# The edge loops of stages 1 and 5, staggered by a pair of groups and issued in written order

## The chip, the cores and the metric

The kernel runs on one core of a Trainium2 chip. A core has engines that each run their own stream of instructions in order: TensorE (PE: matmuls, and PEld: its weight loads), VectorE (DVE), ScalarE (ACT), GpSimd (POOL) and SyncE (SP). POOL issues the indirect DMAs (gathers and scatters) here, SP and ACT the plain DMAs. The metric is device microseconds of one launch of the whole program. The edge loops that are changed are two parts of it.

## The reference, cut to what matters

Eight stages run one after the other on 6250 nodes (49 tiles of 128) and a graph of 100000 edges: four graph layers (stages 1, 3, 5, 7), each followed by an expert layer (stages 2, 4, 6, 8). Stage 4's graph has 131072 edges of its own. The edges of stages 1 and 5 are sorted by their target node `dst`. Stage 1 is attention with 4 heads of 64 columns, stage 5 has one head of 256 columns. For each target node both compute a softmax over its edges and a weighted sum of rows of the source nodes:

```
stage 1:  s[e,h] = sum_c q[dst[e],h,c] * k[src[e],h,c] / 8        value row v[src[e]]
stage 5:  s[e]   = leaky(a_src[src[e]] + a_dst[dst[e]] + a_e[e])  value row z[src[e]]
m[n]   = max over e with dst[e] = n of s[e]
p[e]   = exp(s[e] - m[dst[e]])
out[n] = sum p[e] * value[src[e]] / sum p[e]
```

## The kernel before, in words

**Windows.** `windows` (called once) cuts the sorted edges into NW = 112 groups ("windows") of GE = 896 = 7 x 128 edges. A window's first target is `n0`; the targets of its edges lie in `n0` to `n0 + 127` (the seldom case that they do not is handled by `further`, behind a condition). An edge's `lane` is its target minus `n0`. The tables kept in SBUF are `idx` (source nodes), `lane` and `isl` (1 where an edge is the last of its target in the window); in DRAM `laned` (lanes), `rfd` and `rrd` (a very negative number where a target starts, forward and backward) and `isd`.

**The edge loop** is `att_windows` (line 625), used by stage 1 (line 947, table `kvd`, 512 columns) and stage 5 (line 1711, table `zd`, 257 columns). It goes over 56 pairs of windows, `g = 0, 2, ...`:

- `begin` (647): SP loads the lanes, broadcast to all partitions (`lr`); DVE compares them with the partition number to `ohT` (target by edge, bf16, line 745) and builds `oh` (edge by target, bf16, both windows in one instruction, line 654); SP loads the four reset rows `rst`. Then for each window POOL gathers 7 x 128 rows into `roww` (line 603), and `front` makes the scores. In stage 1 `front` (930) spreads the targets' `q` over the edges by 21 matmuls with `ohT` (`qe`, 938), multiplies into the row (941) and reduces (942). In stage 5 (1697) 7 small matmuls `de` do this for one number per target.
- `middle` (672): the scores of both windows are transposed to rows (681, 682: once forward and once reversed), copied by ACT to `sT` (683), and one DVE scan (685) makes running maxima over each target, forward and backward. They are transposed back (688), the backward half turned by 7 matmuls with `flip` (694); the larger of the two is the target's maximum `mxw`. `p` is the exp of the difference (699). `p` goes behind the row's 256 value columns (702), and the maximum times `isl` behind that (703): a sum over a target's edges then delivers its maximum.
- `end` (707): each of the 7 blocks of a row is scaled by `p`, 5 by ACT (715, one instruction per head) and 2 by DVE (718); ACT casts `oh` to f32 `ow` (721); 7 matmuls (725, two passes each in f32) sum the window into one PSUM tile `ops`; ACT copies it out (`osb`, 728); SP stores lanes 1 to 127 to `main` and lane 0 to `part` (749, 750).

For each pair the program calls `begin` and `middle` of the pair and then `end` of the pair before. The order of the instructions on POOL is the written one (`tc.manual_schedule` with POOL alone); on PE, DVE, ACT and SP a scheduler orders them. `roww` has 5 buffers in stage 1 and 6 in stage 5. `att_join` (829) afterwards adds the lane-0 rows of `part` to `main`, with the maxima that stand in the rows' last columns.

**The steps.** `bucket_move` (line 146) sorts another edge list into buckets; it is a generator that yields between small pieces ("steps"). Stage 1 calls it for `sb` (100000 edges, BT = 4) and advances it 3 steps for each window, with the rest after the loop; stage 3 calls it for `sc` (131072 edges, BT = 6), one step for each of 448 chunks. Its phases: counting (49 buckets; compare `isb` and matmul, 224), positions (49 buckets; compare, three matmuls 300 and 302, masked copy 304), moving (groups of columns; per step the one-hots `ol` (321) and `orr` (323, 326) and BT matmuls `mv` (329); at the end of a group some 12 small instructions and 16 scatters by POOL, line 365, 4 a step), and reading back (376 to 389).

## Time and profile before

| what | us |
|---|---|
| median of 3 runs | 11532.18 (11513.21 to 11543.58) |
| the profiled execution | 11636.83 |
| its span in the profile | 11635.0 |
| mean granted TensorE clock | 0.699 of full |
| PE busy | 6837.3 (59%) |
| DVE busy | 5143.1 (44%) |
| POOL busy | 4453.4 (38%) |
| ACT busy | 2537.3 (22%) |

The profile is one execution of the program, recorded by the hardware. Its span is what lies between the first and the last recorded instruction; the profiled execution's own time is the span and 1.8 us around it. An engine's busy time counts its data instructions alone. The clock is what the throttle granted to TensorE; at a lower clock the same matmul takes longer. "Idle before" in a group of instructions is the time its engine stood still just before them, with what released it. [...]

### The profile page before, as it was taken

Reading aid. Unit: us, or ns where it says so; the run is one execution under the profiler, and the core shown is the slowest. Engines: PE = TensorE matmul, PEld = TensorE weight load, DVE = VectorE, ACT = ScalarE, POOL = GpSimd, SP = SyncE. Lnnn points to the kernel's source line nnn. Section 1 sums busy time; section 2 is a strip of 40 time slices with the busy share of each in tenths; the row PEclk is TensorE's granted clock in tenths of the full one; section 3 lists DMA queues with packets and bytes.
Section 4 is the critical chain, followed back from the end, with each engine's and each line's share of the span. In section 5 each row is a group of like instructions: output and inputs, shape, how many; then the busy total and the mean of one; then the engine's idle time right before and its main releaser. Section 6 shows DMA issues by size and latency. Waiting matters only on the chain. (4 is left out here: it accounts for less than half of the span.)

```text
span 11635.0 us, 111114 instructions
## 1 busy us (share of the span) xinstructions
PE 6837.3 (59%) x33823; PEld 4547.9 (39%) x33823; DVE 5143.1 (44%) x14128; ACT 2537.3 (22%) x6685; POOL 4453.4 (38%) x4496
## 2 busy tenths in 40 slices
PE   4787666624866876554555555693455553562295
PEld 2444444423652333333333332481344442351263
DVE  5556565666224655414555555414222223624304
ACT  1344344421222000001111111131233332121021
POOL 0344445410133666662444443123444442053211
PEclk9878777765988766655655555797666666586597
DMA  3444444432653433351000000274333332273122
GB/s 131 160 134 127 133 132 121 133 110 97 204 175 106 119 94 96 108 133 35 7 6 6 6 6 6 89 218 122 94 90 88 88 88 69 87 218 55 47 71 72
DMA packets 613608, 1129.18 MB, mean 97 GB/s; under 512 B 156007, under 2 KB 419750, under 8 KB 598910
## 3 DMA queue, kind: packets, MB, share of 16 engines
q0 software_dynamic: 234752, 600.19, 19.4%
q1 hardware_dynamic: 320159, 454.55, 12.9%
q10 hardware_dynamic: 58060, 66.90, 1.8%
q8 instruction: 284, 4.65, 0.2%
q14 instruction: 353, 2.89, 0.1%
HBM read 930.68 MB, written 190.55 MB: 96 GB/s over the span
## 5 line engine op out<-in xcount | busy, mean ns | idle before, releaser
L603 POOL DMA_INDIRECT roww<-kvd,saidx x784 | 828.3, 1057 | 1145.9 <-ACT osb L728 459.8
L603 POOL DMA_INDIRECT row<-gatd,scsl x864 | 828.2, 959 | 1072.5 <-DVE pv L1463 290.8
L603 POOL DMA_INDIRECT roww<-zd,saidx x784 | 748.0, 954 | 1024.4 <-ACT osb L728 613.5
L603 POOL DMA_INDIRECT row<-w1d,sbsl x896 | 890.0, 993 | 626.7 <-PE nbp L1021 239.3
L725 PE MATMUL ops<-roww,ow 128*128 128x264 f32 (+1 forms) x3136 | 1064.1, 482 | 60.7 <-ACT osb L728 20.2
L715 ACT ACTIVATE roww<-roww,pw 128x64 f32<-128x64 f32 (+1 forms) x2800 | 808.4, 368 | 48.3 <-issue 46.1
L1021 PE MATMUL nbp<-row,sel 128*128 128x256 bf16 x2688 | 586.4, 369 | 382.7 <-DMA row<-w1d,sbsl 222.8
L725 PEld LDWEIGHTS ops<-roww,ow 128*128 128x128 f32 x3136 | 688.3, 238 | 272.2 <-issue 57.5
L1423 DVE TENSOR_REDUCE Mc<-P 128x4 f32<-128x1024 f32 x432 | 520.4, 1221 | 433.6 <-remote 315.0
L938 PE MATMUL qe<-qw,ohT 128*128 128x256 bf16 x2352 | 423.9, 332 | 397.9 <-DVE roww L941 343.0
L329 PE MATMUL mv<-orr,ol 128*128 128x234 f16 (+1 forms) x1824 | 545.1, 444 | 145.6 <-DVE orr L326 108.2
L1021 PEld LDWEIGHTS <-sel 128*128 128x128 bf16 x2688 | 377.5, 155 | 634.6 <-issue 424.2
L1419 PE MATMUL P<-identb,mb 128*128 128x512 bf16 x864 | 473.6, 570 | 190.7 <-issue 66.7
L688 PE MATMUL sm<-ident,sc 64*128 64x64 f32 x784 | 96.2, 283 | 819.1 <-DVE sc L685 756.3
L1260 PE MATMUL yp<-wr,hr 128*128 128x256 f32 x2176 | 535.8, 386 | 52.3 <-DVE yr L1263 52.3
L1298 PE MATMUL hp<-xr,wr 128*128 128x256 f32 x2176 | 534.7, 397 | 27.2 <-ACT hr L1300 19.9
L1057 PE MATMUL tps<-ident,xn 128*128 128x128 f32 x490 | 125.5, 404 | 685.8 <-DVE xn L124 469.8
L1422 PE MATMUL P<-rb,sel 96*128 96x512 bf16 x864 | 471.5, 568 | 89.9 <-DVE rb L1413 76.0
L1263 DVE TENSOR_TENSOR yr<-yp,br 128x256 f32<-128x256 f32 x328 | 138.9, 424 | 859.5 <-PE yp L1260 802.2
L941 DVE TENSOR_TENSOR roww<-roww,qe 128x512 f32<-128x512 f32 x448 | 270.7, 615 | 476.3 <-DMA roww<-kvd,saidx 213.5
L938 PEld LDWEIGHTS <-ohT 128*128 128x128 bf16 x2352 | 262.4, 116 | 535.8 <-issue 303.3
L685 DVE TENSOR_TENSOR_SCAN sc<-rst,sT 64x896 f32<-64x896 bf16 x112 | 225.9, 2017 | 552.3 <-ACT sT L683 503.4
(582 smaller groups left out, 14260.9 us busy)
## 6 DMA issues: line engine op xcount, KB each, us to landing
wr<-in_moe_dram SPq DMA_DIRECT2D x108, 1026.0 KB
lr<-salaned SPq DMA_DIRECT2D x112, 448.0 KB
yd<-yr SPq DMA_DIRECT2D x164, 256.0 KB
wr<-in_moe_dram SPq DMA_DIRECT2D x56, 513.0 KB
eat<-in_edge_attr_dram ACTq DMA_DIRECT2D x32, 781.2 KB
qw<-qd SPq DMA_DIRECT2D x112, 192.0 KB
br<-in_L_ffn_b_dram SPq DMA_DIRECT2D x164, 128.0 KB
main<-osb SPq DMA_DIRECT2D x112, 131.0 KB
```

Of the source, the lines that this page charges most:

```text
L329: nc.tensor.matmul(mv, ol[:, :, i], orr[:, 0:2, :, i], start=(c + i == c0), stop=(c + i == c0 + n - 1))
L603: return self.nc.gpsimd.indirect_dma_start(out=out, out_offset=None, in_=table, in_offset=bass.IndirectOffsetOnAxis(ap=idx, axis=0))
L715: nc.scalar.activation(x, x, AF.Copy, scale=p[:, j, i * H + h:i * H + h + 1])
L725: nc.tensor.matmul(ps[:, :VW], ow[:, j, :], row[:, j, v0:v0 + VW], start=(j == 0), stop=(j == BW - 1))
L938: nc.tensor.matmul(ps[:, b], ohT[:, j + b, :], qw[:, k], start=(k == 0), stop=(k == 2))
L941: nc.vector.tensor_mul(kr, kr, ps[:, :m])
L1021: nc.tensor.matmul(ps, sel[:, :, 2 * (c % G) + k], row[:, j * D:(j + 1) * D], start=(k + j == 0), stop=(k == 1 and j == 2))
L1260: nc.tensor.matmul(yp, hT[:, k, i * 128:(i + 1) * 128], w[:, O2 + k * D:O2 + (k + 1) * D], start=(k == 0), stop=(k == KH - 1))
L1298: nc.tensor.matmul(hp, w[:, k * H + m * 128:k * H + (m + 1) * 128], xe[:, k], start=(k == 0), stop=(k == 1))
L1419: nc.tensor.matmul(P[:, k], mb[:, :, 2 * i + k], self.identb.unsqueeze(1).to_broadcast([128, 4, 128]), start=True, stop=False)
L1422: nc.tensor.matmul(P[:, k], sel[:, 2 * i + k, :], rb, start=False, stop=True)
L1423: nc.vector.tensor_reduce(mg[:, i, :], P.rearrange("p k h e -> p h k e"), AX.XY, ALU.max)
```

## The change

**The loop's order.** `begin` is split into the loads (`begin`, now only SP), the lane one-hots (`lanes`) and the gathers with the scores of one window (`first`); `middle` into `turned` (transposes and `sT`), `scan` and `weigh`; `end` into `scaled` and `sums`. The main loop calls them so that scan, weights and sums of pair k-1 stand inside the iteration of pair k, between the scores of its two windows, and the loads for pair k+1 are issued in it too. `turned` of pair k ends the iteration. All five engines now issue in written order (`ORDERED`). Stage 1 has 6 row buffers. `qw` and `dw` are loaded by `load` with the pair, in 3 and 4 buffers.

**p on the one-hots.** In stage 5 the row is no longer scaled. DVE builds `ow` in f32 from the lane, times `p`, in 7 instructions a window; a column of ones in the table `zd` (now 258 wide) delivers the sum of `p`. In stage 1 ACT scales all 7 blocks and DVE builds `ow` in f32 with one compare. The bf16 `oh` and the cast go.

**Maxima.** Instead of carrying every target's maximum through the sums, the maximum of the first edge and of the last edge of each window is kept in `mfl` and stored once (`ends`). `main` and `part` become narrower, `isl` and `isd` go. `att_join` finds by a matmul with `bef` the maximum of the target that ends a window. The backward half of the scan is transposed back by itself, in reversed order, so that a single matmul turns it.

**The steps.** They are advanced by `tick` at 15 places a pair in stage 1: before each of the four groups of `qe` in both windows, once in `weigh`, and after every second block of `sums`. In `bucket_move` positions yield twice a bucket and the masked copy is put off by one piece; the end of a group is cut into more steps; the scatters are put off and go out one a step; reading back has more steps. This holds for stage 3 too, which otherwise is unchanged.

The diff, cut to its core:

```diff
+ORDERED = {mybir.EngineType.Pool, mybir.EngineType.PE, mybir.EngineType.DVE,
+           mybir.EngineType.Activation, mybir.EngineType.SP}
...
                 for j in range(2):
                     nc.tensor.matmul(big[:, :n], idt[:NT, j, b:b + 1].to_broadcast([NT, 128]),
                                      first[:, j, h:h + n], start=False, stop=(j == 1))
-                nc.vector.copy_predicated(pos[:, h:h + n], q.bitcast(I16), big[:, :n])
-            yield
+                if held is not None:
+                    nc.vector.copy_predicated(*held)
+                held = (pos[:, h:h + n], q.bitcast(I16), big[:, :n])
+                yield
+        nc.vector.copy_predicated(*held)
...
+        late = []
+
+        def scatter(n):
+
+            for _ in range(min(n, len(late))):
+                ti, vt, j = late.pop(0)
+                s = nc.gpsimd.indirect_dma_start(
+                    out=sld, out_offset=bass.IndirectOffsetOnAxis(ap=ti[:W, j:j + 1], axis=0),
+                    in_=vt[:W, 8 * j:8 * j + 8], in_offset=None, bounds_check=NB * 16 - 1,
+                    oob_is_err=False)
+                tc.declare_no_dep(s.ins, group=nm + "sc", reason="each piece has slots of its own")
+                tc.add_to_no_dep_group(nm + "sc", s.ins)
+
...
                 for i in range(k):
                     nc.tensor.matmul(mv, ol[:, :, i], orr[:, 0:2, :, i], start=(c + i == c0),
                                      stop=(c + i == c0 + n - 1))
+                if c > c0:
+                    scatter(1)
                 yield
...
+            st["node"] = [load(r, wp) for r in q["n0"]]
             return st
 
-        def middle(st):
-
-            n, s, q = st["n"], st["s"], st["q"]
-            m = n * H
-            sT = wp.tile([64, GE], F, name="sT", bufs=1)
+        def lanes(st):
+            st["ohT"] = wp.tile([128, 2 * BW, 128], BF, name="ohT")
+            st["q"]["ohT"](st["ohT"].rearrange("p b e -> p (b e)"), st["lr"])
+
+        def first(st, i, half=lambda: None):
+
+            row = gp.tile([128, BW, max(gw, v0 + VW)], F, name="roww")
+            for j in range(BW):
+                self.gather(row[:, j, :gw], tab, st["q"]["idx"](i, j))
+            front(st, i, row, st["ohT"][:, i * BW:(i + 1) * BW], st["s"][:, :, i * H:(i + 1) * H],
+                  wp, sp, tick, half)
+            st["row"].append(row)
+
+        def turned(st):
+
+            s = st["s"]
+            sT = st["sT"] = wp.tile([64, GE], F, name="sT", bufs=1)
             for j0, j1 in ((0, 4), (4, BW)):
                 ps = pm.tile([64, 512], F, name="sm")
                 for j in range(j0, j1):
...
                     nc.tensor.matmul(ps[0:32, o], s[:, j], self.ident, start=True, stop=True)
                     nc.tensor.matmul(ps[32:64, o], s[:, BW - 1 - j], self.flip, start=True, stop=True)
                 nc.scalar.activation(sT[:, j0 * 128:j1 * 128], ps[:, :(j1 - j0) * 128], AF.Copy)
...
+        def scan(st):
+
+            sc = st["sc"] = wp.tile([64, GE], F, name="sc", bufs=1)
+            nc.vector.tensor_tensor_scan(sc, st["rst"], st["sT"], NEG, op0=ALU.add, op1=ALU.max)
+
+        def weigh(st):
+
+            n, s, q, sc = st["n"], st["s"], st["q"], st["sc"]
+            m = n * H
+
             zf = sp.tile([128, 2, BW, m], F, name="zf")
-            for h in range(2):
-                nc.scalar.activation(zf[:, h], zp[:, :, 32 * h:32 * h + m], AF.Copy)
+            for h, r in ((1, slice(32, 64)), (0, slice(0, 32))):
+                zp = pm.tile([128, BW, 32], F, name="sm")
+                for j in range(BW):
+                    nc.tensor.transpose(zp[:, j if h == 0 else BW - 1 - j, :],
+                                        sc[r, j * 128:(j + 1) * 128], self.ident[r, r])
+                nc.scalar.activation(zf[:, h], zp[:, :, 0:m], AF.Copy)
             zr = pm.tile([128, BW, m], F, name="sm")
-            for j in range(BW):
-                nc.tensor.matmul(zr[:, j, :], self.flip, zf[:, 1, BW - 1 - j, :], start=True, stop=True)
+            nc.tensor.matmul(zr, self.flip, zf[:, 1], start=True, stop=True)
+            tick()
             mx = sp.tile([128, BW, m], F, name="mxw")
             nc.vector.tensor_max(mx, zf[:, 0], zr)
-            p = sp.tile([128, BW, m], F, name="pw")
+            p = st["p"] = sp.tile([128, BW, m], F, name="pw")
             nc.vector.tensor_sub(p, s[:, :, 0:m], mx)
             nc.scalar.activation(p, p, AF.Exp)
-            for i in range(n):
-                row, hs = st["row"][i], slice(i * H, (i + 1) * H)
-                nc.vector.tensor_copy(row[:, :, v0 + 256:v0 + 256 + H], p[:, :, hs])
-                nc.vector.tensor_mul(row[:, :, v0 + 256 + H:v0 + VW], mx[:, :, hs],
-                                     q["isl"](i).unsqueeze(2).to_broadcast([128, BW, H]))
-            st["p"] = p
-
-        def end(st):
-
-            for i in range(st["n"]):
-                row, p = st["row"][i], st["p"]
+            for e, j in ((0, 0), (1, BW - 1)):
+                nc.vector.tensor_copy(mfl[:, e, q["at"]:q["at"] + n, :].rearrange("p n h -> p (n h)"),
+                                      mx[:, j, :])
+
+        def scaled(st, i):
+
+            row, p, lane = st["row"][i], st["p"], st["q"]["lane"](i)
+            ow = wp.tile([128, BW, 128], F, name="ow")
+            if H > 1:
+                nc.vector.tensor_tensor(ow, self.iota.unsqueeze(1).to_broadcast([128, BW, 128]),
+                                        lane.unsqueeze(2).to_broadcast([128, BW, 128]), ALU.is_equal)
+                nc.vector.tensor_copy(row[:, :, v0 + 256:v0 + VW], p[:, :, i * H:(i + 1) * H])
                 for j in range(BW):
-                    if j < BW - dve:
-                        for h in range(H):
-                            x = row[:, j, v0 + h * C:v0 + (h + 1) * C]
-                            nc.scalar.activation(x, x, AF.Copy, scale=p[:, j, i * H + h:i * H + h + 1])
-                    else:
-                        x = row[:, j, v0:v0 + 256].rearrange("p (h c) -> p h c", h=H)
-                        nc.vector.tensor_mul(x, x, p[:, j, i * H:(i + 1) * H].unsqueeze(2).to_broadcast(
-                            [128, H, C]))
-                ow = wp.tile([128, BW, 128], F, name="ow")
-                nc.scalar.activation(ow, st["oh"][:, :, i * BW:(i + 1) * BW].rearrange("p n j -> p j n"),
-                                     AF.Copy)
-                ps = po.tile([128, 512], F, name="ops")
+                    for h in range(H):
+                        x = row[:, j, v0 + h * C:v0 + (h + 1) * C]
+                        nc.scalar.activation(x, x, AF.Copy, scale=p[:, j, i * H + h:i * H + h + 1])
+            else:
                 for j in range(BW):
-                    nc.tensor.matmul(ps[:, :VW], ow[:, j, :], row[:, j, v0:v0 + VW], start=(j == 0),
-                                     stop=(j == BW - 1))
-                o = wp.tile([128, VW], F, name="osb")
-                nc.scalar.activation(o, ps[:, :VW], AF.Copy)
-                st["q"]["put"](i, o)
-
-        pid = self.pid
-        held, regs = None, None
-        for g in range(0, NW, 2):
+                    nc.vector.tensor_scalar(ow[:, j], self.iota, lane[:, j:j + 1], p[:, j, i:i + 1],
+                                            op0=ALU.is_equal, op1=ALU.mult)
+            st.setdefault("ow", []).append(ow)
+
+        def sums(st, i):
+
+            row, ow = st["row"][i], st["ow"][i]
+            ps = po.tile([128, 512], F, name="ops")
+            for j in range(BW):
+                nc.tensor.matmul(ps[:, :VW], ow[:, j, :], row[:, j, v0:v0 + VW], start=(j == 0),
+                                 stop=(j == BW - 1))
+                if j % 2:
+                    tick()
+            o = wp.tile([128, VW], F, name="osb")
+            nc.scalar.activation(o, ps[:, :VW], AF.Copy)
+            st["q"]["put"](i, o)
...
+        held, nxt = None, windows(0)
+        lanes(nxt)
+        for g in range(0, NW, 2):
+            st = nxt
+            first(st, 0, (lambda: scan(held)) if held is not None else (lambda: None))
+            if g + 2 < NW:
+                nxt = windows(g + 2)
             if held is not None:
-                end(held)
+                weigh(held)
+                scaled(held, 0)
+            if st["n"] > 1:
+                first(st, 1)
+            if held is not None:
+                if held["n"] > 1:
+                    scaled(held, 1)
+                for i in range(held["n"]):
+                    sums(held, i)
+            turned(st)
+            if g + 2 < NW:
+                lanes(nxt)
             held = st
-        end(held)
+        scan(held)
+        weigh(held)
+        for i in range(held["n"]):
+            scaled(held, i)
+            sums(held, i)
         for _ in steps:
             pass
+        for e, r in ((0, slice(0, 1)), (1, slice(127, 128))):
+            nc.sync.dma_start(ends[e:e + 1], mfl[r, e, 0:NW, :])
...
+        bef = wp.tile([NW, NW], F, name="ajbe")
+        nc.vector.tensor_scalar(bef, t[:NW, :NW], S["lastf"], None, op0=ALU.is_equal)
+        nc.vector.tensor_tensor(bef, bef, eq, ALU.is_gt)
...
+            def load(n0, wp):
+                qw = wp.tile([128, 3, D], BF, name="qw", bufs=3)
+                nc.sync.dma_start(qw, qd[ds(n0, 128), :].rearrange("p (j d) -> p j d", j=3))
+                return qw
+
+            def front(st, i, row, ohT, s, wp, sp, tick, half):
+                qw = st["node"][i]
                 for j in range(0, BW, 2):
+                    tick()
+                    if j == 4:
+                        half()
                     m = min(2, BW - j)
                     ps = pq.tile([128, 2, D], F, name="qe")
                     for b in range(m):
...
                                         AX.X, ALU.add)
 
             steps = other(cx)
-            with tc.manual_schedule(engines={mybir.EngineType.Pool}):
-                self.att_windows(cx, S, kvd, 512, 4, 256, front, main, part, rows=5, steps=steps, per=3)
+            with tc.manual_schedule(engines=ORDERED):
+                self.att_windows(cx, S, kvd, 512, 4, 256, load, front, main, part, ends, rows=6, steps=steps)
...
+                    z = wp.tile([128, 258], F, name="z")
+                    nc.scalar.activation(z[:, 1:257], zp[:, D:], AF.Copy)
+                    nc.vector.memset(z[:, 257:258], 1.0)
                     for i, o in enumerate((z[:, 0:1], DD[:, t:t + 1])):
```

## The prediction

> **What bounds the kernel now.** I read the table of busy time by stretch first, cut at the first and last instructions on `roww`: the stage 1 edge loop runs from 380 to 2475 us, that of stage 5 from 8134 to 9811 us. Together they are 3772 of 11635 us; the rest is touched only in the helper `bucket_move`.
>
> ```profile
> core 0: us, PE busy (x) PEld busy (x) DVE busy (x) ACT busy (x) POOL busy (x), PEclk, DMA share, GB/s
> 380.00:2475.00 2095.00, 1436.24 (x7930) 958.45 (x7928) 1225.33 (x2550) 880.84 (x2765) 977.77 (x899) 0.76 0.44 131
> 8134.00:9811.00 1677.00, 860.88 (x5098) 705.61 (x5098) 381.14 (x1181) 544.59 (x1065) 747.99 (x784) 0.67 0.32 86
> ```
>
> No engine is full in either: 69% for PE in the first, 51% in the second. So both loops are chains of waits, not throughput. 56 pairs of windows: 2095/56 = 37.4 us and 1677/56 = 29.9 us a pair. Next, the waits inside 48 steady pairs of stage 5 (us in total, times, longest), and one pair in the timeline (start, us, engine):
>
> ```profile
> PEld sm L688 <- DVE sc L685: 667.0, 48, 14.9
> ...
> POOL roww L603 <- ACT osb L728: 569.0, 48, 12.2
> DVE e L1705 <- DMA roww<-zd,saidx: 432.0, 45, 14.0
> ```
> ```profile
> 8507.82 1.01 POOL L603 DMA_INDIRECT roww<-zd,saidx  x1 [11.90 <-ACT osb L728]
> ...
> 8524.12 0.95 POOL L603 DMA_INDIRECT roww<-zd,saidx  x1 [0.30 <-issue]
> 8527.82 0.48 ACT L683 ACTIVATE sT<-sm 64x384 f32<-64x384 f32 x1 [9.01 <-remote]
> ...
> 8528.34 2.02 DVE L685 TENSOR_TENSOR_SCAN sc<-rst,sT 64x896 f32<-64x896 bf16 x1 [8.46 <-ACT sT L683]
> ...
> 8530.41 1.00 PE L688 MATMUL sm<-ident,sc 64*128 64x64 f32 x7 [13.83 <-DVE sc L685]
> ...
> 8532.37 2.99 PE L694 MATMUL sm<-zf,flip 128*128 128x2 f32 x14
> ...
> 8537.17 1.01 POOL L603 DMA_INDIRECT roww<-zd,saidx  x1 [12.10 <-ACT osb L728]
> ```
>
> The reader sees a ring: 14 gathers at 0.95 + 0.30 us issue take 17.3 us (8507.82 to 8525.07); then the data, the scan, its transposes and 14 flips; only then do the old pair's last sums leave PE and free a row buffer for the next gather. 8537.17 - 8507.82 = 29.35 us, of which POOL idles 12. The gathers and the softmax take turns.
>
> Stage 1 has the same ring, but shares DVE and PE with `bucket_move` (lines 321 to 329), whose steps are slipped between its instructions by the scheduler. The groups of 700 to 2300 us (busy, mean ns) and a step as it ran:
>
> ```profile
> L603 POOL DMA_INDIRECT roww<-kvd,saidx x596 | 638.4, 1071 | 589.9 <-ACT osb L728 393.6 <-issue 163.7 <-ACT roww L715 22.1
> ...
> L329 PE MATMUL mv<-orr,ol 128*128 128x230 f16 x742 | 183.0, 383 | 35.7 <-DVE orr L326 25.1 <-issue 8.9
> L941 DVE TENSOR_TENSOR roww<-roww,qe 128x512 f32<-128x512 f32 x257 | 173.9, 681 | 325.3 <-DMA roww<-kvd,saidx 175.3 <-remote 123.6 <-PE qe L938 7.4
> L942 DVE TENSOR_REDUCE ss<-roww 128x28 f32<-128x1792 f32 x85 | 170.9, 2011 | 0.0
> ...
> L326 DVE TENSOR_TENSOR orr<-orr,v 128x460 f16<-128x460 f16 x362 | 150.0, 446 | 0.3
> ```
> ```profile
> 1500.39 7.74 ACT L715 ACTIVATE roww<-roww,pw 128x64 f32<-128x64 f32 x32
> ...
> 1505.51 1.47 PE L938 MATMUL qe<-qw,ohT 128*128 128x256 bf16 x12
> ...
> 1513.23 0.98 PE L329 MATMUL mv<-orr,ol 128*128 128x230 f16 x4
> ```
>
> So a 64-column scaling costs 0.242 us in a row, `qe` 0.1225, and a step's four `mv` 0.98.
>
> **Stage 5, part by part.** The stagger takes scan, weights and sums of pair k-1 into the iteration of pair k; with 6 row buffers POOL may then gather up to a pair ahead, so the landing and the scan leave its ring. Its own floor is 14 x 1.25 = 17.5 us a pair. In written order PE's iteration is a chain; latencies of 0.05 to 0.15 us between engines are read off the timeline. `de` and its reduce 0.9; scan 2.05; two sets of 7 transposes, 1.0 each (the rows of L688) 2.0; one flip instead of 7 (2 of the 14 passes of 2.99 us) 0.5; maximum, difference, exp 0.85; first one-hot 0.4; sums of window 0, 14 passes at 0.30 (0.354 in this stage at clock 0.67, 0.25 in the fastest run of stage 1), 4.5; copy out before the single accumulator is free, 0.5; window 1, 4.5; the 28 transposes of `turned`, 1.7 (8512.48 to 8514.20). Sum 17.9. Against POOL's 17.5 I take 19.0 for jitter between two such close bounds. New work that lies beside it: 14 DVE one-hots with p. The nearest rows are a 64-column tensor_scalar with one column operand, 0.247 us (L1802), and a 256-column one with two, 0.396 (L124); nearer the second in operands and between them in length, 0.33. That is 2.3 us a window, less than PE's 4.5 for the same sums, so it hides; at 0.396 it still does. The ACT scalings (5 x 0.497 a window), the 1.81 us casts (L721), the DVE `oh` (1.09) and four products of 0.417 go; none is the last to end now, so they save nothing by themselves. 56 x 19 + 35 for fill and drain = 1099, against 1677: **-578 us**. Ends: 17.5 a pair gives -662.
>
> From the other side: gathers are made on POOL while DVE writes. Where DVE is 58% busy (stage 1) a gather means 1071 ns, in stage 5 951 at 23%. If the one-hots cost each gather those 0.12 us, POOL needs 14 x 1.37 = 19.2 us, near what I take. If POOL stood still for all of DVE's one-hot time (14 x 0.33 + `ohT` 0.69 = 5.3 us) a pair takes 22.8 us, gain 366. I keep 22.8 as the high end.
>
> [...]
>
> **Stage 1.** Without steps: PE starts `qe` at 0; DVE multiplies at 0.95, 1.65, scans (2.4 to 4.4, placed after the second product), multiplies, reduces until 7.5. Only then come maximum, difference and exp (8.5), because DVE goes in order. ACT now scales all 7 blocks: 28 x 0.242 = 6.8 us a window, both windows before the first copy out: 8.5 + 13.6 + 0.4 = 22.5. The second window's sums wait for that copy: +4.3, `turned` +1.6: **28.5 us** a pair. POOL needs 14 x 1.37 = 19.2 and is hidden. The one-hot compare, 1.0 us a window on DVE, lies under ACT.
>
> With steps: 15 places a pair (4 + 4 in the fronts, 1 in the weights, 6 in the sums) instead of 6, so the order of instructions has counting in pairs 0 to 4, positions in 4 to 11, `mv` in 11 to 27, the rest to 31, and then 25 bare pairs. But in written order a step's four `mv` stand before the `qe` of the same place, and the `mv` wait for the step's own DVE work: ol, orr and two products, 0.43 + 0.39 + 0.70 uncontended, 0.48 + 0.45 + 0.89 by the means; 1.7. So DVE does 1.7, waits 0.1 + 0.98 + 0.78 + 0.15 for `mv` and `qe`, and multiplies 0.68: 4.4 us a place, where 0.7 was needed. A front is 3 x 4.4 + 3.7 + 2.0 = 18.9 (the first, its step done early, 17.2). Pair: 17.2 + 3.8 (step, maximum, exp, one-hot) + 18.9, PE then starts the sums at 37.3, six steps of 1.0 between 8.4 us of sums, one wait of 2.6 for the step after DVE's one-hot, a copy out, `turned`: **58 us**. A place costs (58 - 28.5)/15 = 2.0 us. With counting and positions (two 0.28 us compares, or one and a deferred masked copy, and 0.5 to 0.75 us of PE) the place in a front is 2.5: pair 41.
>
> Places: 49 + 98 at 41: 9.8 pairs, 402. 203 with `mv`: 13.5 pairs at 58, 783. About 116 light ones at 31: 7.7 pairs, 239. 25 bare at 28.5: 713. Sum 2137. The set-up of the steps, formerly ahead of the loop, now waits for its two loads inside it: 30. Seven groups each put two ACT copies behind the scalings, and DVE waits some 3 us for each: 40. Fill and drain 35. Total 2242 against 2095: **+147 us**. Ends: if a place costs only DVE's own time (15 x 1.7 + 14.9, 42 a pair with fill; 34, 29 and 27 for the other three kinds) 1868, -227; if the places in the sums cost more (70; 50, 34, 31) 2577, +480.
>
> **The rest, together.** Stage 3 runs the same steps under the scheduler, 455 instead of 321 over 448 chunks; its steps now reach chunk 403 instead of 323. Its chunks take 4.1 us with `mv` (188 from 4042 to 4820) and 3.05 without steps (140 to 5245), and the deferred copy may remove the 78.8 us that L304 waited for L302. Ends +86 (80 chunks more at the 1.1 us between) and -79; the middle, +4. SP: the loads of lane rows, reset rows and nodes move ahead of the previous pair's stores; the reset rows already waited for the scan (536 us over 48 pairs) and nobody waited for SP; a store now queues behind them by some 2 us of issue, and its reader is the join: nothing. `ends` (two short stores, one load), `bef` and its matmul: some 3 us once, against one store and 7 casts of `isl` gone: nothing. The 112 scatters, 1.32 + 0.3 us, now go one a step between gathers; POOL has 58 - 19 us free there.
>
> Sum: -578 + 147 + 4 = -427. The profiled execution took 11636.8 us (1.8 outside the span), 0.9% above the median of 11532.2. 11636.8 - 427 = 11209.8, times 0.991: **11109 us**, 3.7% less. The rivals' times are scaled alike.
>
> **The rivals.**
> 1. Slower: the lockstep of `mv` and `qe` in stage 1, pairs 11 to 27. It has to eat stage 5's 578 us: 203 places at 3.7 us (every place costs what one in a front does) and 147 at 2.0 make 1596 + 751 + 294 + 105 = 2746, +651, total +77: 11608. It decides from 3.4 us a place. For it: DVE and PE share no slack there by order. Against: 7 of 15 places stand where ACT or PE is awaited anyway.
> 2. The stagger works better: stage 5 at POOL's 17.5, stage 1 at DVE's own time: -662 - 227 + 4: 10655. For it: both are sums of rows. Against: PE's chain in stage 5 is as long as POOL's.
> 3. POOL is held by the new one-hots: 22.8 in stage 5, stage 1 as I have it: -366 + 147 + 4, 11319.
> 4. The order brings nothing in stage 5 since the row buffers still bind, 29.4 us a pair: 147 + 4, 11682. Against: gathers of pair k need the sums of pair k-3, which PE ends in iteration k-2.
>
> **How the numbers follow.** Forecast 0.55, rival 1 0.10, rival 2 0.14, rival 3 0.18, rival 4 0.03. Rivals 1 and 4 are slower. 0.3% (35 us) is about what a measurement here can tell. Range: low 10700, near rival 2; high, rival 3 with stage 1 midway to its high end (+310) is -52: 11480. Faster 0.86, same 0.02, slower 0.12.
>
> **What would show it.** Right: a stage 5 loop near 1100 us with POOL at 65% or more and a pair of 18 to 20 us; in stage 1 pairs of about 58 us between the first and last `mv`, PE waiting for `orr` in front of `qe`, and 28 us after. Wrong: gathers well above 1 us in stage 5 (rival 3), POOL idle by over 5 us a pair there (rival 4), or `mv` pairs near 42 (rival 2) or 70 (rival 1).

## The result and the profile after

The changed kernel takes 11887.64 us (median of 4, 11861.61 to 11905.29) against 11532.48 for the kernel before (median of 4): 1.031 times as long, 95% interval 1.028 to 1.033. It is slower by 3.1%, where 3.7% faster was forecast. The profiled execution took 11874.9 us, 238 more than that of before. Cut at the first matmul of a loop's front and the last of its sums, the two profiles differ like this:

| stretch | before, us | after, us | difference | forecast |
|---|---|---|---|---|
| stage 1 edge loop | 2068 | 2454 | +386 | +147 |
| stage 3, chunk loop | 1584 | 1519 | -65 | +4 |
| stage 5 edge loop | 1635 | 1638 | +3 | -578 |
| the rest | 6348 | 6262 | -86 | 0 |

Of the rest, 71 us lie between stages 3 and 5, where nothing was changed; two later profiles taken side by side had 2918 and 2898 us there, so this is scatter. 16 us are the steps' set-up, now inside the loop. My -578 and +147 were taken from 1677 and 2095 us, the loops cut at the first and last work on `roww`; by the cut of this table the same forecasts of 1099 and 2242 us are -536 and +174.

The table of busy time by stretch of the kernel after: both loops, and between them three parts of stage 1 (up to the first `mv`, up to the last, the rest).

```profile
core 0: us, PE busy (x) PEld busy (x) DVE busy (x) ACT busy (x) POOL busy (x), PEclk, DMA share, GB/s
380.00:2834.00 2454.00, 1493.62 (x7640) 962.46 (x7638) 1249.67 (x2395) 898.22 (x3545) 950.58 (x895) 0.68 0.38 111
380.00:988.00 608.00, 383.05 (x1558) 181.66 (x1557) 266.21 (x571) 161.56 (x631) 159.54 (x167) 0.60 0.31 94
988.00:1894.00 906.00, 511.96 (x2650) 339.05 (x2650) 562.22 (x1179) 252.39 (x994) 343.73 (x313) 0.64 0.30 84
1894.00:2834.00 940.00, 598.62 (x3434) 441.74 (x3432) 421.24 (x647) 484.27 (x1921) 447.32 (x415) 0.78 0.50 148
8392.00:10030.00 1638.00, 711.56 (x4811) 571.60 (x4808) 438.96 (x1567) 136.91 (x392) 742.55 (x782) 0.67 0.33 88
```

In stage 5 ACT fell from 545 to 137 us of work and PE from 861 to 712, and the loop is no shorter. POOL is busy 45% of it; I had said 65% or more. The waits inside some 50 of its pairs (us in total, times, longest), and one pair in the timeline:

```profile
DVE e L1802 <- remote: 762.1, 40, 22.0
POOL roww L631 <- PE ops L766: 583.1, 50, 15.5
...
ACT sT L712 <- remote: 267.5, 49, 7.2
```
```profile
9006.93 0.94 POOL L631 DMA_INDIRECT roww<-zd,saidx  x1 [10.62 <-PE ops L766]
9007.15 0.27 SPq L795 DMA_DIRECT2D main<-osb  x1
9007.18 3.31 PE L766 MATMUL ops<-roww,ow 128*128 128x257 f32 x14 [0.53 <-ACT osb L771]
...
9012.07 0.33 PE L1800 MATMUL de<-dw,ohT 128*128 128x3 bf16 x7
9012.63 0.59 ACT L712 ACTIVATE sT<-sm 64x512 f32<-64x512 f32 x1 [1.67 <-PE de L1800]
...
9016.87 0.48 ACT L712 ACTIVATE sT<-sm 64x384 f32<-64x384 f32 x1 [3.65 <-remote]
...
9022.49 0.18 DVE L1802 TENSOR_REDUCE e<-de 128x7 f32<-128x21 f32 x1 [16.71 <-remote]
9022.67 2.02 DVE L717 TENSOR_TENSOR_SCAN sc<-rst,sT 64x896 f32<-64x896 bf16 x1
9023.19 2.25 POOL L631 DMA_INDIRECT roww<-zd,saidx  x1 [0.30 <-issue]
```

Up to 9012.4 everything goes at the pace of my chain. Then `de` is recorded as done at 9012.40, and its only reader on DVE starts at 9022.49. Ten microseconds are lost there, while POOL makes the pair's 14 gathers (9006.9 to 9025.4). By the records of the whole loop the reader starts 10 to 14 us behind the pair's first `de` in 52 of 56 pairs. So the scan, the weights and the sums of a pair begin only when the burst of gathers is nearly over, and POOL then waits 10.6 us for the sums (its line at 9006.93): gathers and softmax still take turns, 29.2 us a pair. "remote" means that the awaited semaphore rose at that moment, but no instruction was recorded near it that raised it. The `[9.01 <-remote]` ahead of `sT` among my lines of before was the same thing: in that profile 96 signals of the transposes ahead of `sT` (L682) came late, half of them by 12.7 us or more.

Stage 1's two groups on the page (busy, mean ns, idle before) show the lockstep that I had forecast:

```profile
L348 PE MATMUL mv<-orr,ol 128*128 128x234 f16 (+1 forms) x1824 | 545.5, 444 | 472.4 <-DVE orr L345 423.2
...
L1033 DVE TENSOR_TENSOR roww<-roww,qe 128x512 f32<-128x512 f32 x448 | 269.1, 615 | 997.1 <-PE qe L1030 729.5
```

### The profile page after: what moved, and what is told of

Read it like the earlier page. It is cut to its first block, busy times and chain, and to the rows that moved or that the text cites. A ratio compares the mean times of both kernels' runs of the same rounds, so it can differ in the third digit from the quotient of the medians.

```text
span 11873.1 us, 110708 instructions
## 1 busy us (share of the span) xinstructions
PE 6737.9 (57%) x33267; PEld 4416.9 (37%) x33267; DVE 5223.9 (44%) x14399; ACT 2148.7 (18%) x6797; POOL 4445.3 (37%) x4496
## 5 line engine op out<-in xcount | busy, mean ns | idle before, releaser
L766 PE MATMUL ops<-roww,ow 128*128 128x260 f32 (+1 forms) x3136 | 1064.6, 497 | 277.1 <-ACT osb L771 160.9
L766 PEld LDWEIGHTS ops<-roww,ow 128*128 128x128 f32 x3136 | 759.4, 254 | 523.1 <-ACT osb L771 206.5
L754 ACT ACTIVATE roww<-roww,pw 128x64 f32<-128x64 f32 x3136 | 755.1, 333 | 2.0
L728 PE MATMUL sm<-ident,sc 32*128 32x32 f32 x1568 | 134.1, 278 | 861.9 <-DVE e L1804 560.2
L1030 PE MATMUL qe<-qw,ohT 128*128 128x256 bf16 x2352 | 453.3, 353 | 120.0 <-DVE roww L1033 99.1
L348 PEld LDWEIGHTS <-ol 128*128 128x128 f16 x1824 | 227.6, 126 | 716.1 <-issue 399.9
```

Of the source, the lines that this page charges most:

```text
L348: nc.tensor.matmul(mv, ol[:, :, i], orr[:, 0:2, :, i], start=(c + i == c0), stop=(c + i == c0 + n - 1))
L754: nc.scalar.activation(x, x, AF.Copy, scale=p[:, j, i * H + h:i * H + h + 1])
L766: nc.tensor.matmul(ps[:, :VW], ow[:, j, :], row[:, j, v0:v0 + VW], start=(j == 0), stop=(j == BW - 1))
L1030: nc.tensor.matmul(ps[:, b], ohT[:, j + b, :], qw[:, k], start=(k == 0), stop=(k == 2))
```

## The experiments

Two questions stood open. What delays TensorE's readers in stage 5? And does the lockstep cost what stage 1 lost? The kernels ran in five sets, each on one chip beside the kernel before. Times in the table are of one execution each, and medians of four for `pool_order_t`, `after_c` and `pool_order_d`; the last column's are medians of seven in sets 4 and 5. Where a kernel carries one edit in stage 1 and one in stage 5, each is read in its own loop.

How a late signal is counted: the trace holds the times at which TensorE's semaphore rose and the ends of the matmuls that raise it. A signal is late when it comes over 1 us behind the end of the last such matmul. The stage 5 loops (late signals of all, in the recorded part):

| kernel (set) | stage 1, us | stage 5, us | late in stage 5 | time, us | before in the set |
|---|---|---|---|---|---|
| before (prediction's profile) | 2068 | 1635 | 99 of 672 | 11636.8 | |
| after (result's profile) | 2454 | 1638 | 101 of 1151 | 11874.9 | |
| `s5_narrow` (1) | 2263 | 1079 | 0 of 1175 | 10629 | 10262 |
| `s5_none` (1) | 2246 | 945 | 0 of 1175 | 10470 | 10262 |
| `s1_steps_first` (1) | 1618 | 1107 | 0 of 1174 | 10606 | 10262 |
| `s1_tick_late` (1) | 1947 | 1108 | 0 of 1175 | 10329 | 10262 |
| `before_b` (2) | 2069 | 1634 | 109 of 681 | 11648 | 11640 |
| `after_b` (2) | 2480 | 1722 | 121 of 1129 | 12058 | 11640 |
| `pool_order` (2) | 1985 | 1267 | 103 of 1167 | 11125 | 11640 |
| `narrow_late` (3) | 2261 | 1537 | 161 of 979 | 11660 | 11656 |
| `none_first` (3) | 1687 | 949 | 0 of 1176 | 11113 | 11656 |
| `turn_late` (3) | 2239 | 1593 | 200 of 1078 | 11701 | 11656 |
| `before_narrow` (3) | 2055 | 1279 | 291 of 950 | 11277 | 11656 |
| `before_c` (4) | 1740 | 1219 | 0 of 788 | 10256 | 10256 |
| `pool_order_t` (4) | 1777 | 1111 | 0 of 1176 | 10177 | 10256 |
| `pool_late` (4) | 1785 | 1115 | 0 of 1178 | 10180 | 10256 |
| `pool_busy` (4) | 2248 | 1157 | 0 of 1174 | 10678 | 10256 |
| `pool_busy_b` (5) | 2498 | 1157 | 0 of 1176 | 11520 | 11630 |
| `after_c` (5) | 2505 | 1730 | 131 of 1138 | 12096 | 11630 |
| `pool_order_d` (5) | 1971 | 1264 | 114 of 1160 | 11119 | 11630 |

TensorE's signals were late in the first profiles and in sets 2, 3 and 5, and in neither loop of any kernel of sets 1 and 4. This is not a matter of the chip, since sets 1 and 5 ran on one chip and sets 2 and 4 on another. Nor does the granted clock tell the two apart: the stage 5 loop had 0.76 in `s1_tick_late` (set 1), with no signal late, and 0.76 in `pool_order_d` (set 5), with 114 late. Comparisons below stay inside one of these two conditions, unless they are between them.

### Set 1: less or no gathering in stage 5; stage 1's loop alone; the step in another place

`s5_narrow` (rows in six buffers that are set to zero once) and `s5_none` (no gather at all):

```diff
-                self.gather(row[:, j, :gw], tab, st["q"]["idx"](i, j))
+                self.gather(row[:, j, :8], tab, st["q"]["idx"](i, j))
```

> Stage 5 as changed, but every gather brings 8 of 258 columns (32 bytes a row instead of 1032) into row buffers that are set to zero once, so this leaves the values out of the sums. The number of gathers, the rows of each and all instructions on the other engines stay. In the profile of the changed kernel the pair takes 27.5 us and TensorE's completions of `turned` and `de` come 5 to 10 us behind their records, in the time of the gathers. Theory A, the rows' bytes that land in SBUF hold TensorE up: the delay goes, the pair comes to the 18 to 19 us of my chain, the loop to 1050 to 1100 us (was about 1660). Theory B, the making of the descriptors on POOL holds it up: 14 gathers still take 17.5 us, the delay stays, the loop stays above 1550 us.

> Stage 5 as changed, but without any gather in the loop (row buffers set to zero once), so this leaves the values out. Theories A and B alike: without gathers nothing delays TensorE, the pair is the chain of 17.9 us and the loop 1000 to 1050 us. Theory C, the delay has nothing to do with the gathers (loads and stores of SP, the clock): the pair stays at 25 us or more, the loop above 1400 us.

`s1_steps_first`:

```diff
             with tc.manual_schedule(engines=ORDERED):
+                for _ in steps:
+                    pass
-                self.att_windows(..., rows=6, steps=steps)
+                self.att_windows(..., rows=6)
```

> Stage 1 as changed, but all steps of `bucket_move` are run before the edge loop, none in it. It measures the bare loop: I forecast 28.5 us a pair, 56 of them and 35 us of ends: 1631 us. If the loop itself, and not the steps, is what was sized wrong, it takes 1800 us or more; then TensorE must be late in the gathers here too. If it is near 1631, the 385 us that stage 1 lost belong to the places where steps and loop meet.

`s1_tick_late`:

```diff
                 for j in range(0, BW, 2):
-                    tick()
                     if j == 4:
                         half()
...
                             nc.tensor.matmul(ps[:, b], ohT[:, j + b, :], qw[:, k], ...)
+                    tick()
                     kr = row[:, j:j + m, 0:D]
                     nc.vector.tensor_mul(kr, kr, ps[:, :m])
```

> Stage 1 as changed, but in a front the step comes between the matmuls of `qe` and the product that reads them, instead of in front of `qe`: a step's `mv` then stand behind the `qe` of their own place, and VectorE makes the next one-hots while TensorE works. Stage 3 does not have this place and stays. Theory lockstep: a place in a front falls from some 4.4 us to 2.4, 8 places a pair: -16 us over 16 `mv` pairs, about -8 over 12 counting and position pairs: the loop falls from 2485 to about 2130 us. Rival, the gathers or ScalarE set the pair: less than 80 us change.

The surprise was that kernels with stage 5 untouched ran its loop in 1107 us, 19.8 us a pair, where the first profile had 1638: no signal was late, so the gathers' bytes could not be tested here (1079 with few, 945 with none, where 1000 to 1050 was expected of the chain alone). The forecast had been 1099. The same place in a pair of `s1_tick_late`, stage 5 as changed:

```profile
7913.15 0.96 POOL L631 DMA_INDIRECT roww<-zd,saidx  x1 [0.30 <-issue]
7913.56 0.32 PE L1800 MATMUL de<-dw,ohT 128*128 128x3 bf16 x7 [2.68 <-DMA dw<-ddd]
7913.91 0.18 DVE L1802 TENSOR_REDUCE e<-de 128x7 f32<-128x21 f32 x1 [0.61 <-PE de L1800]
7914.09 2.02 DVE L717 TENSOR_TENSOR_SCAN sc<-rst,sT 64x896 f32<-64x896 bf16 x1
7914.41 2.45 POOL L631 DMA_INDIRECT roww<-zd,saidx  x1 [0.30 <-issue]
...
7919.67 1.03 POOL L631 DMA_INDIRECT roww<-zd,saidx  x1 [0.30 <-issue]
```

Here the reduce starts as `de` ends (7913.88), in the middle of the same burst of gathers. The loop's row:

```profile
7382.00:8490.00 1108.00, 715.42 (x4816) 575.82 (x4813) 461.02 (x1567) 126.29 (x392) 809.58 (x782) 0.76 0.47 131
```

With 0.30 us of issue ahead of each gather, POOL is taken for some 1044 of these 1108 us: 18.6 us a pair. So it is POOL that sets the pair here, while the chain without gathers takes 945/56 = 16.9. Stage 1's bare loop takes 1618 us, 28.9 a pair (forecast 28.5). The loop with steps takes 2246 to 2263 (forecast 2242). Moving the step behind `qe` brings 308 us, of some 350 expected of the lockstep. Two groups in the `mv` part of stage 1, first of `s5_narrow`, whose stage 1 is as changed, then of `s1_tick_late`:

```profile
L348 PE MATMUL mv<-orr,ol 128*128 128x230 f16 x800 | 198.2, 382 | 326.2 <-DVE orr L345 326.2
L1045 DVE TENSOR_TENSOR roww<-roww,qe 128x512 f32<-128x512 f32 x125 | 77.4, 621 | 232.2 <-PE qe L1042 232.2
```
```profile
L348 PE MATMUL mv<-orr,ol 128*128 128x230 f16 x799 | 198.0, 382 | 167.6 <-DVE orr L345 167.0
...
L1033 DVE TENSOR_TENSOR roww<-roww,qe 128x512 f32<-128x512 f32 x126 | 77.7, 617 | 50.7 <-PE qe L1029 50.7
```

DVE's wait for `qe` falls from 232 to 51 us, PE's for the one-hots by half.

### Set 2: both kernels again, and POOL alone in written order

```diff
-ORDERED = {mybir.EngineType.Pool, mybir.EngineType.PE, mybir.EngineType.DVE,
-           mybir.EngineType.Activation, mybir.EngineType.SP}
+ORDERED = {mybir.EngineType.Pool}
```

> The kernel before once more, unchanged, for its trace beside those of the changed kernel on one and the same chip. On the chip of the first experiments the kernel before took 10262 us instead of 11532, and the changed stage 5 loop 1107 us instead of 1638, the changed stage 1 loop 2250 instead of 2454: near my forecasts of 1099 and 2242 on that chip. Theory chip: TensorE's delay in the gathers, seen in the first two traces, is a matter of the chip, and it lengthened the old loops more than mine were allowed for: here the two old loops come to some 2900 us together (3703 in the first trace). Rival: the old loops are as long as before and the 1270 us came off elsewhere; then the changed kernel is faster on this chip.

> The changed kernel once more, unchanged, on the same chip as the other runs of this set. On a chip without TensorE's delay: stage 1 loop 2250, stage 5 loop 1107, together about 10650 us and slower than before by 3 to 4%. On one with the delay: 2454 and 1638.

> The changed kernel, but only POOL issues in written order; PE, DVE, ACT and SP are left to the scheduler, as in the kernel before. Theory lockstep: in written order a step's `mv` hold up `qe`; the scheduler puts ready work between, so the pairs with steps get shorter: stage 1 loop 250 us or more below the changed kernel's in this set, stage 5 within 60 us of it. Rival, the staggered loop itself (7 scalings on ACT, one accumulator) is what costs: stage 1 within 80 us of the changed kernel's.

This set had the late signals, so the theory of a kind of chip was open again and set 4 ended it. `before_b` repeated the first profile; `after_b` came 84 us above the 1638 expected of its stage 5 loop. `pool_order` gained in both loops: 495 us in stage 1, twice my bound, and 455 in stage 5, where I had expected no more than 60. The row order of one window's sums in its trace shows what is late, the matmul or its signal (us; not lines of the profile):

```
matmuls that signal, ends:  8809.51 8810.37 8811.23 8812.08 8812.94 8813.80 8814.33
semaphore rises:            8813.49 8813.53 8813.57 8813.61 8813.66 8813.81 8814.34
```

Six of these seven signals fell due 0.86 us apart. The first five were held for 0.7 to 4.0 us and came 0.04 us apart. The shortest that 14 passes of 257 columns took in the traces shown is 3.31 us, 0.24 us each, at a granted clock of 1.00 (the line at 9007.18 of the result's profile). Matmuls of two such passes did not run 0.04 us apart: the work was done, its signals were late.

### Set 3: bytes or descriptors, and another order

`narrow_late` and `none_first` join edits of set 1. `turn_late` has the step behind `qe` and, in stage 5:

```diff
+                if H == 1:
+                    turned(st)
                 for i in range(held["n"]):
                     sums(held, i)
-            turned(st)
+            if held is None or H > 1:
+                turned(st)
...
-                    nc.vector.tensor_reduce(e[:, 0], ps, AX.X, ALU.add)
                     half()
+                    nc.vector.tensor_reduce(e[:, 0], ps, AX.X, ALU.add)
```

`before_narrow` is the edit of `s5_narrow` in the kernel before.

> Two edits that do not meet, one a stage: the 8-column gathers in stage 5 (leaves the values out of the sums) and the step between `qe` and its product in stage 1. On a chip where TensorE's completions come late: theory A (bytes that land), stage 5 loop 1050 to 1150 us instead of 1640 to 1720; theory B (descriptors), above 1500. Stage 1: lockstep alone would take 300 us off the 2454 to 2480; if the delay of TensorE in the gathers also sits in the places, less than 200. On a chip without the delay: 1080 and 1947 as measured there.

> Two edits that do not meet: no gathers in the stage 5 loop (leaves the values out), and all steps before the loop in stage 1. On a chip with the delay: stage 5 loop 950 to 1000 us if the gathers alone bring the delay (945 without it), above 1200 if TensorE is slow there without gathers too. Stage 1's bare loop, which keeps its gathers: 1618 us on the chip without the delay; here above 1700 if the delay reaches it.

> Two edits that do not meet, all engines still in written order. Stage 5: `turned` of pair k is issued before the sums of pair k-1 instead of behind them, and the scan before the reduce of `de`, so scores and scan no longer wait for the sums. Stage 1: the step between `qe` and its product. With the delay: the delay of `turned` lies beside the wait for the first one-hots, stage 5 falls from 1640-1720 to about 1270 us, what the scheduler's order reached. If it stays above 1500, the scheduler's gain had another source. Without the delay: 1107 to about 1070, POOL's 17.5 us a pair and the jitter.

> The kernel before, with 8-column gathers in stage 5 (leaves the values out). On a chip with TensorE's delay: if the old stage 5 loop of 1635 us was also lengthened by it, it falls by 300 us or more, towards the ring of POOL's 17.5 us and some 6 us of softmax and sums, 1300 us; if its 29.9 us a pair were the ring alone, as the prediction read it, it stays above 1550. On a chip without: this run's untouched stage 1 shows what the old loop of 2068 us takes there.

With late signals, gathers of 8 columns keep most of the delay (1537 us, 161 late signals). Its waits in 1480 us of the loop, and the row of the loop without gathers:

```profile
DVE e L1814 <- remote: 912.9, 53, 18.6
...
ACT sT L724 <- remote: 552.0, 99, 11.0
```
```profile
8320.00:9269.00 949.00, 703.03 (x4816) 559.84 (x4816) 444.20 (x1568) 135.50 (x393) 0.00 (x0) 0.80 0.16 43
```

Without gathers the delay is gone to the last signal, and 949 us are the 945 of set 1. So most of it does not need the bytes. Stage 1's bare loop pays only 69 us for the condition (1687 against 1618). The step behind `qe` brings 193 to 241 us in the stage 1 loops of `narrow_late` and `turn_late` (2261 and 2239, against 2454 and 2480), less than the 300 expected of the lockstep alone and less than the 308 without late signals. `turn_late` missed in stage 5 by 320 us: moving `turned` out of the burst moved other handoffs of TensorE into it, and those became late. Its timeline in one burst:

```profile
8900.58 0.18 ACT L730 ACTIVATE zf<-sm 128x14 f32<-128x14 f32 x1 [3.09 <-remote]
...
8905.64 0.17 DVE L735 TENSOR_TENSOR mxw<-zf,sm 128x14 f32<-128x14 f32 x1 [7.55 <-remote]
...
8913.48 0.18 DVE L1806 TENSOR_REDUCE e<-de 128x7 f32<-128x21 f32 x1 [5.20 <-remote]
```

`before_narrow` came to the number expected (1279 against 1634), but its signals were as late as ever (291), so it does not show that the delay went: DVE's wait for the rows to land is shorter too, 482 us in some 50 pairs of `before_b` and 259 here. It is inconclusive on the delay.

### Set 4: the kernel before without late signals, POOL alone in order timed, fills for gathers

`pool_late` adds the edit of `s1_tick_late` to `pool_order`. `pool_busy` replaces each gather of stage 5:

```diff
-                self.gather(row[:, j, :gw], tab, st["q"]["idx"](i, j))
+                for _ in range(4):
+                    nc.gpsimd.memset(row[:, j, :], 0.0)
```

> The kernel before, unchanged, for its trace on this call's chip. On a chip without the delay: the two old loops together 2900 us instead of 3703, most of the gain in stage 5 (1634 to about 1150, POOL's ring without the late handoffs) and the rest in stage 1 (2069 to about 1750). On a chip with the delay: 2069 and 1634 again.

> The changed kernel with POOL alone in written order, as in the kernel before, now timed in rounds. One look gave 11125 us against 11640. Theory: with the delay of TensorE's completions it is 4 to 5% faster than the kernel before, as the scheduler lets fewer handoffs of TensorE stand one behind the other in a burst of gathers. On a chip without the delay I expect the stage 1 gain alone: near the before's 10262 us, within 2%.

> POOL alone in written order, and the step between `qe` and its product. If the scheduler already keeps a step's `mv` from holding up `qe`, the place of the step in the text matters little: stage 1 within 60 us of the 1985 us of the run without this edit. If the written place still rules, stage 1 falls by 100 us or more.

> The changed kernel with stage 5's gathers replaced by four fills each on POOL, into the same row buffer at the same place of the order (leaves the values out). POOL is as busy as with gathers, waits for the same sums and delays the same readers, but there is no indirect DMA. Theory B1, POOL's work as such holds TensorE's signals up: the completions of `turned` and `de` come late by microseconds again. Theory B2, it takes the descriptors of indirect DMAs: no completion is late, as without gathers. On a chip without the delay it shows nothing of this.

The kernel before, without late signals, by stretch (both loops, columns as above):

```profile
394.00:2134.00 1740.00, 1328.66 (x7905) 902.78 (x7904) 1208.93 (x2523) 867.52 (x2759) 995.92 (x894) 0.83 0.51 156
7199.00:8418.00 1219.00, 860.34 (x5096) 705.65 (x5096) 370.73 (x1175) 538.81 (x1064) 816.24 (x775) 0.72 0.42 116
```

The two old loops take 2959 us instead of 3703. So 744 us of what I took for rings of waits was delay, 415 of it in stage 5 (1219 us, where some 1150 was expected). ACT's wait for the scores there, in `before_b` and in `before_c`:

```profile
ACT sT L683 <- remote: 647.8, 95, 11.8
```
```profile
ACT sT L683 <- PE sm L682: 10.4, 46, 0.2
```

The changed kernel's 2255 + 1107 stand against 1740 + 1219: +515 and -112, and with the scatter elsewhere about 10650 against 10256 (worked out from `s5_narrow`, with 1107 in place of its 1079). By that estimate it is slower without late signals too, by 3.8%, and for another reason: stage 1 alone. The unchanged edit of both stages was itself timed only with late signals. `pool_order_t` is 0.8% faster than before (ratio 0.992, 0.990 to 0.994). With a scheduler, the step's place in the text matters little: 1785 against 1777 us.

### Set 5: what brings the delay, and both orders with intervals

> The fills instead of stage 5's gathers once more (leaves the values out). Without the delay the loop takes 1157 us, as measured. With it: theory B1, POOL's work as such, completions of `turned` and `de` late by 4 to 6 us each and the loop above 1500 us; theory B2, the descriptors of indirect DMAs, no completion late in stage 5 (while they are in stages 1 to 4) and the loop below 1200 us.

> The changed kernel, unchanged. Without the delay, from the untouched stages of the other runs: stage 1 loop 2250, stage 5 loop 1107, about 10650 us, 3.8% slower than before's 10256. With it: 11888 to 12058, 3.1 to 3.6% slower.

> POOL alone in written order, unchanged. Without the delay 0.8% faster than before, as measured (10177). With it 11125, 4.4% faster, from one look.

The late signals were back. With fills the stage 5 loop has none, while stage 1 of the same execution, which keeps its gathers, took 2498 us, against 2248 with the same kernel in set 4. Its row by stretch and the waits in 1000 us of it:

```profile
8521.00:9678.00 1157.00, 763.91 (x4816) 603.20 (x4816) 459.33 (x1567) 137.29 (x393) 999.89 (x3110) 0.76 0.13 35
```
```profile
ACT osb L784 <- PE ops L779: 664.4, 98, 9.4
DVE e L1817 <- POOL row L710: 334.6, 91, 6.6
PEld ops L779 <- POOL row L710: 236.9, 98, 4.0
DVE e L1815 <- PE de L1813: 221.2, 48, 6.2
```

POOL is busier than with gathers (1000 us, against 743 in the result's profile and 810 in `s1_tick_late`), and none of the waits is `remote`; the loop takes the same 1157 us in both conditions. In this loop it takes the indirect DMAs, not a busy POOL, to hold TensorE's signals up: 0 of 1176 are late with fills, 131 of 1138 with gathers (`after_c`). `after_c` is 4.0% slower than before (1.040, 1.038 to 1.042), with its 12096 us a little above the 12058 that I gave as the upper end; `pool_order_d` is 4.4% faster (0.956, 0.954 to 0.958). POOL alone in written order beats both kernels in both conditions, the kernel before by 0.8% where no signal is late.

## Why the prediction was wrong

**The baseline.** Both my forecasts of the new loops were sums of records and handoffs of 0.05 to 0.15 us; in total they hold where signals come in time (1099 against 1107 us, 2242 against 2255), in part by luck, as shown below. But I subtracted them from old loops that held 744 us of delay, and with late signals the new loops hold their own. "PE's iteration is a chain; latencies of 0.05 to 0.15 us between engines are read off the timeline" is the step that failed: the first `de` of a pair reached its reader after 10 to 14 us, that of `turned` after up to 7.2. The line with `[9.01 <-remote]` was among those I quoted, and the sum has no term for it. Between the two first profiles the miss is 665 us (+238 against -427). The delay in the new loops is 730 of it: 531 in stage 5 (1638 against 1107) and 199 in stage 1 (2454 against 2255). The different cut (69) and the sizes (8 and 13) add to it; stage 3 (69) and the rest (86) take from it. I read the old 29.9 us a pair as gathers and softmax taking turns; without the delay the same order takes 1219/56 = 21.8.

**Stage 5, -578 forecast, +3 measured.** Without the delay a pair takes 19.8 us, where I took 19.0 for a chain of 17.9 beside POOL's 17.5. The parts were less right than their result: the chain alone takes 16.9, and POOL 18.6, since gathers beside the scan take longer (below). In the chain the sums were too dear: 14 passes at 0.30 us make 4.2 and not the 4.5 a window that I added, and the line at 9007.18 has 3.31. With the delay, signals of both halves of `turned` and of `de` come late one after the other (waits of 268 and 762 us in some 50 pairs of the result's profile), and the written order puts all of them in the burst. The condition costs per pair, from the loops with and without it: 9.5 to 11.1 us in written order (1638, 1722 or 1730 against 1107), 7.4 in the kernel before, 2.7 to 2.8 in POOL's order alone, none without gathers (949 us against 945) or with fills (1157 in both). That the scheduler's order loses less because fewer handoffs of TensorE follow one another in a burst is argued from the timelines; `turn_late`, my attempt to do it by hand, failed, so it is not shown.

**Stage 1, +147 forecast, +386 measured.** The lockstep was right in kind, and near in size for `mv`: 58.5 us a pair (906 us, 15.5 pairs) with late signals and 54.5 without (845 us, `s5_narrow`), against 58. The three parts without late signals are 526, 845 and 892 us. Counting and positions, with their set-up, were sized too low (432), the last part too high (987), and the `mv` part at 823: the sum of 2242 came near 2255 because two errors of some 95 us cancel. (The parts that I listed for the `mv` pair add to some 56.5, not 58.) The sum, 2454 against 2242, lies inside my ends. Without late signals the old loop takes 1740, so the written order costs 515 us there. Of those, 308 come back when the step stands behind `qe`, and 170 more when the scheduler orders it (1777).

**The rest, +4.** Stage 3 became shorter, by 65 and 44 us with late signals (the first profiles and set 2) and by about 40 without (1442 against 1401 to 1407): inside my ends, towards the low one. The deferred copy explains little of it: the idle time before the masked copies in that loop fell by 10 us only (58 to 48, `before_b` and `after_b`). What brought the rest was not tested.

**The rivals.** Rival 1's mechanism (lockstep) was there, at the forecast's price and not its own; it did not need to eat 578 us. Rival 2 did not come: `mv` pairs took 54 to 58 us, not 42. Rival 4 comes closest in time (11682) and has the symptom, POOL idle for `ops` 583 us in some 50 pairs. Its cause is refuted: without late signals six row buffers are enough, and POOL's gathers follow at 0.30 us. Rival 3 is refuted, but not by the 0.95 us that a gather means in the stage 5 loop of the result's profile: there no gather ran beside a new one-hot. In `s1_tick_late` 219 did, with a mean of 0.97 us, against 0.945 for the 397 beside neither the scan nor a one-hot of any kind. So POOL did not stand still during the new one-hots: the 22.8 us a pair of this rival, and of my high end, rested on an assumption that no run shows. Beside the scan, though, single gathers took 2.25 and 2.45 us (the lines at 9023.19 and 7914.41). In `s1_tick_late` 97 gathers ran beside a scan, with a mean of 1.51 us: 0.57 us more than the 397, about one microsecond a pair.

## What to carry to other kernels

A wait that ends by nothing recorded is a cost of its own: price it before the part around it is called a ring, and ask of a forecast built from records whether the baseline holds the same waits. Work that one engine does for a side task should stand in its queue so that no main result is behind an operand that is not made yet (308 us in stage 1 here, without late signals); where that is hard to write out, a scheduler's order was worth 4% (10177 against the estimated 10650 us) to 8% here (11119 against 12096). A profile of the same kernel from another session tells whether such a wait belongs to the kernel: the old stage 5 loop took 1635 us in one and 1219 in another.

## What was not expected of the hardware

TensorE's semaphore signals were held by up to 14 us in the steady stage 5 loop, in and just behind POOL's bursts of indirect DMAs, and in places several then came together, 0.04 us apart. In other sessions on the same two chips none was late by over 1 us in these loops. In stage 5's loop it needs the indirect DMAs (0 of 1176 late with fills, 0 of 1176 without gathers) and mostly not their bytes (161 of 979 late with 32 bytes a row); whether their issue by POOL or the transfers hold the signals was not separated. The kernel before takes 11532 to 11656 us with it and 10256 to 10262 without, 12 to 14% more with it. What turns it on was not found; nothing in the kernel did. The matmuls' records show no such delay (a window's 14 passes take 3.31 us with late signals, at 9007.18, and 3.31 without, at 7905.92 in `s1_tick_late`), but their signals waited, 101 of 1151 by over 1 us in the result's profile: `de` is recorded as done at 9012.40, and its reader started at 9022.49.
